# Products with wv, wq and wk: three float32r products of split operands in place of Strassen steps in float32, with weight parts loaded for each pair and the norms on ScalarE

## The chip, the core and the metric

The kernel runs on one core of one Trainium2 chip. A core has five engines that run side by side, each with its own queue of instructions in a fixed order: TensorE (PE, matrix products into the accumulator memory PSUM), VectorE (DVE) and ScalarE (ACT) for elementwise work, GpSimd (POOL) and SyncE (SP). SP, ACT and POOL also start memory transfers (DMA), which run on 16 DMA engines that all queues share. An instruction at the head of its engine's queue that waits for another engine holds up everything behind it.

The metric is device time in microseconds (us) for one execution of the whole program; less is better. All tiles below have 128 partitions, and "512 elements" means 512 per partition.

## The reference

Two layers on x of 64 batches x 256 rows x 512 columns, each a residual with a layer norm. The first is masked attention with 8 heads, the second a product with the adjacency matrix.

```python
def _L0_gnn_ref(x, adj, Wq, bq, Wk, bk, Wv, bv, Wo, bo):
    q = (x @ Wq + bq).reshape(b, n, H, HD)
    k = (x @ Wk + bk).reshape(b, n, H, HD)
    v = (x @ Wv + bv).reshape(b, n, H, HD)
    scores = jnp.einsum('bqhd,bkhd->bhqk', q, k) / jnp.sqrt(jnp.float32(HD))
    scores = scores + (1.0 - adj)[None, None, :, :] * -1000000000.0
    attn = jax.nn.softmax(scores, axis=-1)
    out = jnp.einsum('bhqk,bkhd->bqhd', attn, v).reshape(b, n, d)
    return out @ Wo + bo

def _L1_gnn_ref(x, adj, weight, bias):
    y = jnp.einsum('nm,bmd->bnd', adj, x)
    return jnp.einsum('bnd,do->bno', y, weight) + bias

x = _layernorm(x + _L0_gnn_ref(x, adj, ...), axis=-1)
x = _layernorm(x + _L1_gnn_ref(x, adj, ...), axis=-1)
```

## The kernel before

**Pairs and windows.** The 64 batches are taken as 32 pairs; a pair has 512 rows. The work is laid out in windows. Window w holds the attention of pair w, the three products with wv, wq, wk for pair w+1, and for pair w-1 the projection with wo, the norm, the product with adj, the product with the second layer's weight, and the second norm. x of pair w+2 is turned round in window w. So in the middle of the run one window costs one pair's time. `between(w)` lists the steps of a window in order, `window(w)` puts four attention units between them: a unit is a `scores` call (16 matmul rows, L309, with exponentials L313 on ScalarE and masks L318 on VectorE) and a `values` call (sums L336, values L344, evacuated by ScalarE as zc and vc). Steps put off work with `later`, which `tick` releases a step or more afterwards. A scheduler then fixes the order on every engine; in the first window TensorE and VectorE keep the order as written, in the last TensorE does.

**Products.** Every product of 512 x 512 x 512 (with wv, wq, wk, wo and the second weight) is done in seven Strassen steps (`SEVEN`, `block_product`, L231). A step is four float32 matmuls of 128x128 with 256 columns; the trace shows each of these as two instructions. The sums that Strassen needs are made on VectorE: `weight_sums` once for each weight, `row_sums` (L191) for x, for the attention's output and for the second layer's input. Results are put together by `assembled`: ScalarE evacuates the first of two contributions (L276 for q and k, L288 for v), VectorE adds the others (L263; L414 onto the residual r). All weights stay in memory.

**The product with adj** (`adj_x`, L453) is not Strassen: r is split into two parts, hl and ys, in float32r, a format that TensorE takes in a single pass. ScalarE makes the first part (L438), VectorE the rest (L439).

**Norms.** `stats` on VectorE (L385, L386), `rstd_of` (L391 on VectorE, then a power on GpSimd, L393), and one step later `normed`: four VectorE instructions of 512 elements for each layer (L400), subtract the mean and multiply. After the first layer's norm hl and ys follow, after the second the output is stored (L403) and the next r is loaded.

**Loads.** x of each pair comes in four chunks, each of four transfers of 64 KB in pieces of 128 bytes (L83, on SP), so that VectorE's 32x32 transposes (L249) finish the turn; the first pair is turned by TensorE (L246). r is one transfer of 1 MB a pair (L88).

**Buffers.** PSUM has four banks for attention (`ps_at`) and four for products (`ps_mm`). A Strassen product holds one bank through most of its steps and a second for a part of them.

Of the kernel before, what the change touches and what calls it, by code (L numbers as in the profile page):

```python
# [21 lines left out]
F32R = mybir.dt.float32r  # L22
AF = mybir.ActivationFunctionType
# [5 lines left out]
EPS = 1e-5  # L29
MASKED = -1000000000.0  # L30
# [10 lines left out]
def fast(tc, x, adj, wq, bq, wk, bk, wv, bv, wo, bo, w1, b1, out):  # L41
# [20 lines left out]
    xpool = pool("xp", 1)  # L62
    two = pool("two", 2)
# [8 lines left out]
    XC, R, XT, Q, K, V, E, SM, O, HL, Y, ST = ({} for _ in range(12))  # L72

    def load_x(p, i):


        if p < NP:
            t = XC[p, i] = xpool.tile([P, D], F32, name=f"x{i}")
            if p == 0:
                nc.sync.dma_start(t, xc[p, i % 2, i // 2])  # L80
            else:
                for q in range(4):
                    nc.sync.dma_start(t[q * 32:(q + 1) * 32].rearrange("i (m j) -> i m j", j=32), xb[p, i, q])  # L83
# [8 lines left out]
    for i in range(4):  # L92
        load_x(0, i)
    ident = cpool.tile([P, P], F32, name="ident")
# [36 lines left out]
    weights("v", wv, "hl", nc.scalar)  # L131

    nc.scalar.activation(small.tile([P, 1], F32, name="table"), ones[:, 0:1], AF.Exp)
    weights("q", wq, "e0", nc.sync)
    bq_s, bk_s = by_partition(bq, "bq"), by_partition(bk, "bk")
    weights("k", wk, "e1", nc.sync)
# [100 lines left out]
    def x_t(p, i):  # L237
        if i == 0:
            t = two.tile([P, NC, DC, 2, P], F32, name="xT")
            XT[p] = dict(t=t, **blocks(t[:, :, 0:2], t[:, :, 2:4]))  # L240
        t = XT[p]["t"]
        xs = XC.pop((p, i))
        if p == 0:
            pt = ps_mm.tile([P, DC, P], F32, name="mm")
            for d in range(DC):
                nc.tensor.transpose(pt[:, d, :], xs[:, d * P:(d + 1) * P], ident)  # L246
            nc.scalar.activation(t[:, i // 2, :, i % 2, :], pt, AF.Copy)
        else:
            nc.vector.transpose(t[:, :, i].rearrange("p c b i -> p b c i"),  # L249
                                xs.rearrange("p (b c i) -> p b c i", b=2, c=NC))  # L250
        load_x(p + 1, i)

    def x_sums(p, i):
        row_sums(XT[p], sums_of("xs"))
# [10 lines left out]
    def q_or_k(p, i, is_k):  # L265
        T, b = (K, bk_s) if is_k else (Q, bq_s)
        pm = block_product("qk"[is_k], i, XT[p], W["qk"[is_k]], True)

        def out(g, c):
            if (p, g) not in T:  # L270
                T[p, g] = qk.tile([P, NC, 2, 2, P], F32, name="kT" if is_k else "qT")
            return T[p, g][:, c].rearrange("p a b i -> p a (b i)")

        def first(to, pm, g):
            for a in range(2):
                nc.scalar.activation(to[:, a], pm[:, a], AF.Identity, bias=b[:, 2 * g + a:2 * g + a + 1])  # L276

        assembled(i, pm, out, first)

    def v_rows(p, i):  # L280
        pm = block_product("v", i, XT[p], W["v"], False)

        def out(g, c):
            if (p, g) not in V:
                V[p, g] = four.tile([P, NC, 2, HF], F32, name="v")
            return V[p, g][:, c]

        assembled(i, pm, out, lambda to, pm, g: nc.scalar.activation(to, pm, AF.Copy))  # L288

    def q_cols(p, i):  # L290
        q_or_k(p, i, False)

    def k_cols(p, i):
        q_or_k(p, i, True)
# [6 lines left out]
    def scores(p, u):  # L301
        g, b = UNITS[u]
        for kc in range(NC):

            sc = [ps_at.tile([P, 2, N], F32, name="at") for s in range(2)]
            for a in range(2):
                for s in range(2):
                    r = slice(s * HD, (s + 1) * HD)
                    nc.tensor.matmul(sc[s][:, a, :], K[p, g][r, kc, a, b, :], Q[p, g][r, :, a, b, :],  # L309
                                     start=True, stop=True)  # L310
# [15 lines left out]
    def values(p, u):  # L326
# [13 lines left out]
        for a in range(2):  # L340
            for kc in range(NC):
                for h in range(4):
                    col = h * HD + a * 32
                    nc.tensor.matmul(at[h * 32:(h + 1) * 32, a, :], V[p, g][:, kc, b, col:col + 32],  # L344
# [5 lines left out]
    def divided(p, u, vc, zc):  # L350
# [7 lines left out]
        rs = one.tile([P, N], F32, name="rs")  # L358
# [29 lines left out]
    def rstd_of(p, layer):  # L388
# [3 lines left out]
        rstd = ST[p, layer, "r"] = small.tile([P, 4], F32, name="rstd")  # L392
        nc.gpsimd.tensor_tensor(rstd, ve, power, op=OP.pow)  # L393

    def normed(p, layer):
        mv, rstd = ST.pop((p, layer)), ST.pop((p, layer, "r"))
        for b in range(2):
            for c in range(NC):
                i = 2 * b + c
                nc.vector.tensor_scalar(R[p][:, b, c, :], R[p][:, b, c, :], mv[:, i, 0:1], rstd[:, i:i + 1],  # L400
                                        op0=OP.subtract, op1=OP.mult)
            if layer:
                nc.sync.dma_start(outr[p, b], R[p][:, b])  # L403
            elif b == 0:
                for half in range(2):
                    split(p, b, half)
# [20 lines left out]
    def split(p, b, half):  # L427
# [13 lines left out]
    def adj_x(p, i):  # L441
# [16 lines left out]
        if p < NP - 2 and b == 0:  # L458
            later(1, split, p, 1, half)
# [13 lines left out]
    def by_batch(p, layer, b, lo, hi):  # L473
        if b == 0:
            if (p - NP) % 2 == layer:
                PART[p, layer] = two.tile([P, NC, DC, 2, P], F32, name="xT").rearrange("p c (h k) b i -> p (c h) k (b i)", k=2)
            else:
                PART[p, layer] = sums_of("yx"[layer] + "s")
        PART[p, layer, b] = row_sums(blocks(lo, hi, b), PART[p, layer][:, :, :, b * P:(b + 1) * P])

    def part(p, layer, b, i):
# [6 lines left out]
        if i >= 5:  # L488
# [9 lines left out]
            later(1, finished, p, layer, b, c, mv, rstd)  # L498

    def finished(p, layer, b, c, mv, rstd):  # L500
        r = R[p][:, b, c]
        nc.vector.tensor_scalar(r, r, mv[:, 0:1], rstd, op0=OP.subtract, op1=OP.mult)  # L502
        if layer:
            nc.sync.dma_start(outr[p, b, :, c], r)
        elif c == 0:
            for half in range(2):
                split(p, b, half)
# [25 lines left out]
    def between(w):  # L533
# [5 lines left out]
        both = lambda m, n: [s for pair in zip(m, n) for s in pair] if m and n else m + n  # L539
# [234 lines left out]
```

## Time and profile before

| | |
|---|---|
| median of 3 runs | 2680.01 us (2677.47 to 2680.05) |
| the profiled execution, its own time | 2678.74 us |
| its span, first to last instruction | 2676.9 us |
| granted TensorE clock, mean | 0.996 |
| a middle window, 1010.21 to 1092.29 us | 82.08 us |
| in it: TensorE, VectorE, ScalarE, GpSimd busy | 82.08, 62.01, 25.44, 4.24 us |
| in it: DMA engines busy, traffic | 18%, 39 GB/s |
| transfers of the program: SP's queue, ACT's queue | 105.69 MB, 1.05 MB |

Busy time is the time in which an engine has at least one instruction running. Instructions of one engine overlap at their ends, so what one costs in a stream is the distance from its start to the next start, which is shorter than its duration. L numbers are lines of the kernel before. In lists of groups, the arrow names what is written and what is read, and "x512" says how many there are; in a timeline the first two columns are start and length, and brackets hold idle time before the row and what ended it. A window of DMA traffic by stages showed 379 GB/s in the stretch from 4 to 10 us, where the first x and weights load. The trace has no transfer from POOL's queue.

### The profile page before, as it was taken

What the parts mean: (1) busy time and instruction counts of PE and PEld (TensorE: products, weight loads), DVE (VectorE), ACT (ScalarE), POOL (GpSimd) and SP (SyncE); (2) the same over time, 40 slices, a digit from 0 to 9 for tenths busy, and PEclk for the clock granted to TensorE, in tenths of its full rate; (3) what the DMA queues carried; (4) which work ended last, traced back from release to release, by engine and by line L of the source; (5) the groups of instructions that cost most, each with busy time, mean ns of one, the idle gap of its engine ahead of it and who ended that gap; (6) DMA issues with size and microseconds to landing.
All of it is one profiled execution on the core that took longest, in us unless ns stands there. A gap on an engine that the chain in (4) does not pass through costs nothing.

```text
span 2676.9 us, 42203 instructions
## 1 busy us (share of the span) xinstructions
PE 2647.6 (99%) x17190; PEld 2167.0 (81%) x17190; DVE 2002.2 (75%) x3315; ACT 818.7 (31%) x1670; POOL 140.6 (5%) x340
## 2 busy tenths in 40 slices
PE   9999999999999999999999999999999999999987
PEld 7788888888888888888888888888888888888866
DVE  5777777777877777777777777787777777777777
ACT  3333332333323333323333233332233332333221
POOL 0000000000000000000000000000000000000001
PEclk9999999999999999999999999999999999999998
DMA  6210122201212102222012220122210122200010
GB/s 166 36 42 9 46 48 48 48 10 39 48 48 48 32 16 48 48 48 47 6 44 48 48 48 23 26 48 48 48 44 9 45 48 48 48 9 25 32 40 25
DMA packets 304583, 109.49 MB, mean 41 GB/s; under 512 B 265472, under 2 KB 270848, under 8 KB 304384
## 3 DMA queue, kind: packets, MB, share of 16 engines
q1 hardware_dynamic: 303296, 105.69, 16.6%
q8 instruction: 137, 2.24, 0.3%
q10 hardware_dynamic: 1088, 1.05, 0.1%
q14 instruction: 62, 0.51, 0.1%
HBM read 73.14 MB, written 33.55 MB: 40 GB/s over the span
## 4 chain that ended last, share of the span: by engine, by line
PE 95%; DVE 3%; DMA 1%; issue 0%; POOL 0%; ACT 0%; ACTq 0%; POOLq 0%; DVEq 0%; SPq 0%
PE mm L231 71%; PE at L309 9%; PE at L344 8%; PE mm L453 5%; PE at L336 3%; DVE e L318 1%; DVE st L491 0%; POOL rstd L497 0%; DVE r L502 0%; DMA hl<-in_L_gnn_Wv_dram 0%; DMA hl<-in_L_gnn_Wo_dram 0%; DMA r<-in_x_dram 0%; DVE r L376 0%; DVE o L360 0%; DVE r L486 0%
## 5 line engine op out<-in xcount | busy, mean ns | idle before, releaser
L318 DVE TENSOR_TENSOR e<-e,adjT 128x1024 f32<-128x1024 f32 x256 | 303.2, 1215 | 53.4 <-ACT e L313 53.4
L263 DVE TENSOR_TENSOR r<-r,mm 128x512 f32<-128x512 f32 (+1 forms) x204 | 133.2, 654 | 229.5 <-PE mm L231 229.1
L313 ACT ACTIVATE e<-at 128x512 f32<-128x512 f32 x512 | 264.8, 602 | 58.8 <-PE at L309 58.5
L276 ACT ACTIVATE kT<-mm,bk 128x256 f32<-128x256 f32 x256 | 107.5, 470 | 495.5 <-PE mm L231 495.5
L309 PE MATMUL at<-qT,kT 64*128 64x256 f32 x2048 | 257.2, 389 | 0.0
L231 PE MATMUL mm<-wo,o 128*128 128x256 f32 x1024 | 243.8, 380 | 3.2 <-DVE o L360 2.5
L309 PEld LDWEIGHTS at<-qT,kT 64*128 64x128 f32 x2048 | 190.7, 186 | 67.6 <-issue 53.3
L344 PE MATMUL at<-e,v 128*32 128x256 f32 x4096 | 245.1, 379 | 0.0
L231 PE MATMUL mm<-xT,wq 128*128 128x256 f32 x1024 | 244.8, 382 | 0.2 <-DVE v L263 0.2
L231 PE MATMUL mm<-xT,wk 128*128 128x256 f32 x1024 | 241.6, 379 | 0.0
L231 PE MATMUL mm<-wv,xT 128*128 128x256 f32 x1024 | 241.4, 384 | 0.0
L231 PE MATMUL mm<-w,o 128*128 128x256 f32 x992 | 235.8, 380 | 0.0
L414 DVE TENSOR_TENSOR r<-r,mm 128x512 f32<-128x512 f32 x240 | 163.0, 679 | 83.7 <-PE mm L231 83.7
L231 PEld LDWEIGHTS mm<-wv,xT 128*128 128x128 f32 x1024 | 192.6, 191 | 35.8 <-issue 10.8
L231 PEld LDWEIGHTS mm<-xT,wq 128*128 128x128 f32 x1024 | 192.0, 190 | 35.1 <-issue 9.6
L231 PEld LDWEIGHTS mm<-wo,o 128*128 128x128 f32 x1024 | 194.7, 190 | 30.6 <-issue 2.9
L231 PEld LDWEIGHTS mm<-xT,wk 128*128 128x128 f32 x1024 | 194.5, 190 | 26.4
L231 PEld LDWEIGHTS mm<-w,o 128*128 128x128 f32 x992 | 186.6, 190 | 24.5 <-DVE xT L191 0.3
L344 PEld LDWEIGHTS at<-e,v 128*32 128x32 f32 x4096 | 133.2, 110 | 88.3 <-issue 0.3
L276 ACT ACTIVATE qT<-mm,bq 128x256 f32<-128x256 f32 x256 | 107.0, 469 | 305.0 <-PE mm L231 305.0
L231 PE MATMUL mm<-wv,xs 128*128 128x256 f32 x768 | 184.5, 383 | 0.0
L231 PE MATMUL mm<-xs,wk 128*128 128x256 f32 x768 | 184.5, 383 | 0.0
(130 smaller groups left out, 3746.2 us busy)
## 6 DMA issues: line engine op xcount, KB each, us to landing
r<-in_x_dram SPq DMA_DIRECT2D x32, 1024.0 KB
x<-in_x_dram SPq DMA_DIRECT2D x496, 64.0 KB
out_dram<-r SPq DMA_DIRECT2D x60, 512.0 KB
out_dram<-r SPq DMA_DIRECT2D x8, 256.0 KB
x<-in_x_dram SPq DMA_DIRECT2D x4, 256.0 KB
wv<-in_L_gnn_Wv_dram ACTq DMA_DIRECT2D x3, 256.0 KB
wq<-in_L_gnn_Wq_dram SPq DMA_DIRECT2D x3, 256.0 KB
wk<-in_L_gnn_Wk_dram SPq DMA_DIRECT2D x3, 256.0 KB
```

What stands on the lines that cost most here:

```text
L231: nc.tensor.matmul(pm[:, j, :], left[:, k, j * P:(j + 1) * P], right[:, k, :], start=begins and j == 0 and k == 0, stop=k == 1, skip_group ...
L263: nc.vector.tensor_tensor(to, to, pm, op=OP.add)
L276: nc.scalar.activation(to[:, a], pm[:, a], AF.Identity, bias=b[:, 2 * g + a:2 * g + a + 1])
L309: nc.tensor.matmul(sc[s][:, a, :], K[p, g][r, kc, a, b, :], Q[p, g][r, :, a, b, :], start=True, stop=True)
L313: nc.scalar.activation(e[:, s], sc[s], AF.Exp, scale=qscale)
L318: nc.vector.tensor_tensor(e, e, mask[:, kc:kc + 1, :].to_broadcast([P, 4, N]), op=OP.mult)
L336: nc.tensor.matmul(at[h * 32:(h + 1) * 32, 0, :], ones, sm[:, h % 2, h // 2, :], start=True, stop=True)
L344: nc.tensor.matmul(at[h * 32:(h + 1) * 32, a, :], V[p, g][:, kc, b, col:col + 32], e[kc][:, h % 2, h // 2, :], start=kc == 0, stop=kc == N ...
L414: assembled(i, pm, out, lambda to, pm, half: nc.vector.tensor_tensor(to, to, pm, op=OP.add))
L453: nc.tensor.matmul(pm[:, j, :], hl[:, i, mc, j * P:(j + 1) * P], adjT[:, mc, :], start=mc == 0 and i == 0, stop=mc == NC - 1 and i == 1)
```

## The change

- **v, q, k.** In place of seven Strassen steps, each product is now three float32r products (`part_products`). Both operands are split (`split`): `cut` keeps the upper bits of a number, `low` is the rest, and `diff` is the number minus 4097 times the rest. The three products are cut x cut, low x (4096 low), and diff x (-diff/4096); the first two are summed in one bank (`near`), the third goes to another (`far`). `joined`: ScalarE evacuates near times (1 + 1/4096), VectorE adds far. A product is four groups (j) of 12 matmuls with 512 columns. The first pair's v is done in plain float32 from wv as it is.
- **x.** After VectorE's transpose, `x_parts` splits each chunk: three VectorE instructions and one on ScalarE. There are four buffers for each kind of part, which is one pair's worth. x passes through three staging buffers (`stage`), and the next chunk is loaded when a chunk has been split.
- **Weights.** `split_w` splits wq, wk, wv in the first window, and the parts are stored in a scratch area of device memory (36 stores of 256 KB on SP). For every pair each of the nine parts (1 MB) is loaded again by POOL's queue into a ring of five buffers (`load_w`); three loads are asked for after v's last group, three after q's, three after k's.
- **Norms.** `normed` and `finished` use ScalarE, with scale rstd and bias `less` = -mean x rstd, which one more small VectorE instruction makes.
- **Order.** `between` is rewritten for the groups. `split` of the kernel before is now called `halves`; some tiles share names and buffers differently (`by_batch`, `zc`).

In the built order of a middle window, the third group of scores stands partly between the first matmuls of q's last group, and part of a values call between k's first two parts and its third.

```diff
+    def load_w(name, p, i):
+        if p < NP:
+            t = wring.tile([P, DC, D], F32R, name="wr")
+            nc.gpsimd.dma_start(t, SCRATCH[name, i])
+            WP[name, p, i] = lambda k: t[:, k]
...
+    def split_w(name, k, p=0):
+        parts = high, low, diff = [WP[name, p, i](k) for i in range(3)]
+        split(WP.pop((name, k)), one.tile([P, D], F32, name="vc"), high, low, diff)
+        load_next()
+        nc.scalar.activation(low, low.bitcast(F32), AF.Copy, scale=FINE)
+        nc.scalar.activation(diff, diff.bitcast(F32), AF.Copy, scale=-1 / FINE)
+        for i, part in enumerate(parts):
+            nc.sync.dma_start(SCRATCH[name, i][:, k], part.bitcast(F32))
+
+    def split(a, cut, high, low, diff):
+        nc.vector.tensor_scalar(cut.bitcast(I32), a.bitcast(I32), -int(FINE), None, op0=OP.bitwise_and)
+        nc.vector.tensor_tensor(low, a, cut, op=OP.subtract)
+        nc.scalar.activation(high, cut, AF.Copy)
+        nc.vector.scalar_tensor_tensor(diff, low.bitcast(F32), -(FINE + 1), a, op0=OP.mult, op1=OP.add)
...
+    def x_parts(p, k):
+        XG[p, k], XL[p, k], XD[p, k] = (parts.tile([P, D], F32R, name=n) for n in ("high", "low", "diff"))
+        cut = XC.pop((p, k)) if p else one.tile([P, D], F32, name="vc")
+        split(XF[p, k], cut, XG[p, k], XL[p, k], XD[p, k])
+        if p:
+            load_next()
...
-    def q_or_k(p, i, is_k):
-        T, b = (K, bk_s) if is_k else (Q, bq_s)
-        pm = block_product("qk"[is_k], i, XT[p], W["qk"[is_k]], True)
...
+    def part_products(name, p, j, rows_first):
+        near, far = (ps_mm.tile([P, D], F32, name="mm") for _ in range(2))
+        for i, (xs, to) in enumerate(((XG, near), (XL, near), (XD, far))):
+            for k in range(DC):
+                a, b = xs[p, k], WP[name, p, i](k)
+                left, right = (a, b) if rows_first else (b, a)
+                nc.tensor.matmul(to, left[:, j * P:(j + 1) * P], right, start=k == 0 and i != 1,
+                                 stop=k == DC - 1 and i != 0)
+        return near, far
+
+    def joined(to, near, far, **kw):
+        nc.scalar.activation(to, near, AF.Identity, scale=1 + 1 / FINE, **kw)
+        nc.vector.tensor_tensor(to, to, far, op=OP.add)
...
-                nc.vector.tensor_scalar(R[p][:, b, c, :], R[p][:, b, c, :], mv[:, i, 0:1], rstd[:, i:i + 1],
-                                        op0=OP.subtract, op1=OP.mult)
+                nc.scalar.activation(R[p][:, b, c, :], R[p][:, b, c, :], AF.Identity, scale=rstd[:, i:i + 1],
+                                     bias=less[:, i:i + 1])
...
-        o, v, q, k = z(o_proj, 7, 1.72), a(v_rows, 7, 1.72), a(q_cols, 7, 1.72), a(k_cols, 7, 1.72)
+        o, l, y = z(o_proj, 7, 1.72), z(last, 7, 1.72), z(adj_x, 4, 0.9)
+        v, q, k = a(v_rows, 4, 2.6), a(q_cols, 4, 2.6), a(k_cols, 4, 2.6)
...
+        after_v = load(("q", 0, 2), ("k", 0, 0), ("k", 0, 1))
+        after_q = load(("k", 0, 2), ("v", 1, 0), ("v", 1, 1))
+        after_k = load(("v", 1, 2), ("q", 1, 0), ("q", 1, 1)) + x_all[2:]
...
+        seq = v[:2] + o[:1] + v[2:3] + o[1:2] + v[3:] + after_v + o[2:3] + q[:1] + o[3:4] + q[1:2] + o[4:] + q[2:] + \
+            after_q + k[:1] + y[:2] + x_steps[:2] + k[1:2] + y[2:] + bo_steps[:1] + l[:1] + k[2:3] + bo_steps[1:]
...
+        return seq + l[1:3] + k[3:] + after_k + l[3:]
```

## The prediction

> **What bounds the kernel now.** I read the page's busy shares, then its chain of waits, then one middle stretch of TensorE's timeline, and ScalarE's and VectorE's timelines beside it.
>
> ```profile
> PE 2647.6 (99%) x17190; PEld 2167.0 (81%) x17190; DVE 2002.2 (75%) x3315; ACT 818.7 (31%) x1670; POOL 140.6 (5%) x340
> PE 95%; DVE 3%; DMA 1%; issue 0%; POOL 0%; ACT 0%; ACTq 0%; POOLq 0%; DVEq 0%; SPq 0%
> ```
>
> TensorE is busy almost throughout and 95% of the chain is its own: time goes if its work goes, as long as no wait takes its place.
>
> ```profile
> 1044.09 1.89 PE L231 MATMUL mm<-xT,wq 128*128 128x256 f32 x8
> 1045.82 1.89 PE L231 MATMUL mm<-xs,wq 128*128 128x256 f32 x8
> 1047.64 0.64 PE L336 MATMUL at<-sm,ones 128*32 128x256 f32 x8
> 1048.09 1.91 PE L344 MATMUL at<-e,v 128*32 128x256 f32 x32
> 1049.93 2.00 PE L309 MATMUL at<-qT,kT 64*128 64x256 f32 x16
> 1051.86 1.99 PE L231 MATMUL mm<-xT,wq 128*128 128x256 f32 x8
> ...
> 1058.43 1.11 PE L453 MATMUL mm<-adjT,ys 128*128 128x256 f32 x8
> 1059.38 1.89 PE L231 MATMUL mm<-w,o 128*128 128x256 f32 x8
> ```
>
> The first column is the start; the next start is the true cost. A Strassen step is 8 instructions in 1.726 us: 0.2157 us each, a "slot". Values cost 2.3 us (L336, L344), scores 1.93. The window from 1010.21 to 1092.29 us, which is one pair in steady state, is 82.08 us.
>
> ```profile
> 1043.29 1.29 DVE L385 BATCH_NORM_STATS2 st<-r 128x6 f32<-128x512 f32 x2
> 1044.83 0.17 DVE L391 TENSOR_SCALAR ve<-mv 128x4 f32<-128x4 f32 x1
> 1046.12 1.92 DVE L400 TENSOR_SCALAR r<-r,mv,rstd 128x512 f32<-128x512 f32 x4 [1.12 <-POOL rstd L393]
> ```
>
> ```profile
> 1047.15 0.63 ACT L438 ACTIVATE hl<-r 128x512 fp32r<-128x512 f32 x1 [2.02 <-DVE r L400]
> 1047.69 0.61 ACT L438 ACTIVATE ys<-r 128x512 fp32r<-128x512 f32 x1
> 1050.13 0.60 ACT L347 ACTIVATE vc<-at 128x512 f32<-128x512 f32 x1 [0.82 <-PE at L344]
> 1051.16 2.06 ACT L313 ACTIVATE e<-at 128x512 f32<-128x512 f32 x4 [0.43 <-PE at L309]
> ```
>
> The last o_proj step ends near 1042.4; the norm starts 3.7 us later on VectorE, hl a further 1.0 us later, and ScalarE is free when vc and the exponentials are due.
>
> **TensorE's work.** Before, one product of 512x512x512 is 7 steps, 56 slots. After, it is 3 x 16 matmuls of 512 columns in float32r. What is one of those worth? A float32 row of 256 columns lasts 382 ns and a float32r row of 256 (L453) 281: 101 ns more, so the float32 row streams about 512 columns and the new matmul is one slot, 48 per product. The other bound is twice the float32r spacing of L453, (1059.38-1058.43)/8 = 0.119, so 0.238; that would hold if streaming and not the weight load set the 0.119. I take 0.2157. q and k save 8 slots for 32 pairs each, v for 31; v of the first pair, plain float32, costs 64 slots: 512 + 248 - 8 = 752 slots, **-162.2 us**, 5.18 us per steady window.
>
> **VectorE, per window.** Starts lie 0.60 us apart for 512 elements, 0.46 for L400. Gone: 8 norms 3.7, 4 xs sums 2.4, 9 adds of L263 5.4. New: 12 joins 7.2, 4 cuts 1.9 to 2.4, 8 differences 4.8, two small ones 0.3. Net +2.7, 62.0 to 64.7 us: covered as a total. **ScalarE** loses 16 L276 at 0.42 and 4 L288 at 0.60, gains 12 evacuations, 4 high parts and 8 norms (0.53 apart): 25.4 to about 30 us, covered too. What costs is order, so I walked one steady window of the built order, each instruction at its start spacing, U = 0 where the last o_proj step ends.
>
> - Norm on ScalarE. Its scale needs `less`, which stands on VectorE behind q's third join (q ends at 2.6): ready at 4.3. ScalarE then runs three norms, hl, ys, the fourth norm (0.53 each) before vc, which was ready at 4.9: vc ends at 8.1. The second half of the scores needs vc's bank; TensorE reaches it at 7.2 and waits **0.94** (0 if ScalarE is quicker, 1.5 if slower).
> - The order splits these scores so that their two row halves no longer run together: 0.97 + 2 x 0.86 for 1.93: **0.76** (0 to 0.86).
> - The exponentials then end at 9.8, the masks 11.75, q's join 12.35, sm 13.6; TensorE wants sm at 12.9: **0.75** (0 to 1.5). Five of its 16 value matmuls are pulled forward, which cuts a group of four: **0.43** (0 to 0.46).
> - wk's third part. Five ring buffers hold nine parts, so its 1 MB load waits on POOL's queue until the last q group has used wq's first part, at 9.45; TensorE wants it at 15.0, 5.55 us later. No POOL transfer is in this trace. The nearest rows: the first x transfer, issued 0.75, used at 3.91 (256 KB; at the 379 GB/s of the stretch 4 to 10 us that is 2.5 us fixed, so 1 MB lands in 5.2), and
>
> ```profile
> 1.74 6.61 DMA hl<-in_L_gnn_Wv_dram
> ```
>
>   256 KB beside 2 MB of others: 6.6 us, 8.7 for 1 MB. I take 6.2, nearer the quiet row since nothing else loads then: **0.65** (0 to 3.2). Behind it in POOL's queue stand two more loads and the small `seen`/`acc`, wanted much later. The other loads have 9 us (wq's third part) or more.
> - VectorE's x parts can only be written once the last k group is done (four buffers each), and they stand between the `last` adds: the sixth `last` step waits **0.6** (0 to 1.5); v's last difference is ready some 1 us ahead. o_proj's first step waits 0.1 for a bank.
>
> Together 4.25 us, of 5.18. For 30 steady windows **+127 us**. Start: 36 stores of parts on SP (about 0.45 us each) stand ahead of the second pair's x, and VectorE splits 12 weight quarters (1.7 us each) plus that x; hoisted scores and values hide most. I take **+8** (0 to 15). Tail: each norm is followed by one more small step, **+2** (-2 to +5). Sum, on the profiled execution's 2678.7 (span 2676.9; median of the runs 2680.0): 2678.7 - 162.2 + 127 + 8 + 2 = **2653.5**.
>
> The Trainium skill speaks twice to wk's load. "DMA: Bandwidth & Descriptors", section "Anatomy of one DMA", gives 2.0 us plus bytes over 436 GB/s, an estimate of 4.4 us for 1 MB: no wait, and the sum would be 2634. Against the change, "SBUF — State Buffer", section "SBUF: two separate sides", says that a transfer issued from GpSimd cannot have its descriptors written while VectorE runs a two-port operation. L400 at 0.54 us against 0.68 for L414 may be such a form, but no run here shows that lock; one cut's 0.46 us in front of each wk load would make the sum 2667.
>
> **Rivals.**
> - *The waits are hidden.* Latencies in this walk are guesses of a tenth or two each, and a later order can absorb them: for it, TensorE now loses under 1 us per window although VectorE is 75% busy. If only the unpaired scores, the cut group and 0.5 us remain (1.7 us): 2678.7 - 162.2 + 51 + 5 = 2573.
> - *wk's third part lands late*, slower than before. TensorE stops in every window before k's first difference product. My sum loses its gain at 25.2/30 = 0.84 us more, a landing of 7.05 us; at 8.7 us it is 2.5 more per window: 2729. For: the load starts on demand, and POOL's share is unseen. Against: 379 GB/s was reached here.
> - *x comes late.* Each pair's fourth x chunk (128-byte pieces) loads while 3 MB of parts go over the same engines; VectorE's transpose would block, then ScalarE's high part, then vc. Some 2.5 us per window: 2729. The walk has 1 to 2 us to spare.
> - *The float32r matmul takes 0.238.* 4560 x 0.022 = +100: 2753. Against: L453's 281 ns.
>
> **Chances.** My forecast 0.42, hidden waits 0.20, late wk 0.24, late x 0.08, 0.238 us 0.06. About 0.2%, 5.4 us, is what a measurement of this kernel can tell from no change. My case spreads some 30 us either way: of its 0.42, 0.31 is faster, 0.06 the same, 0.05 slower. Faster 0.51, same 0.07, slower 0.42. Half of the hidden case lies under 2570 and a tenth in all above 2740, so 2570 to 2740 holds 8 in 10; my own case alone is 2622 to 2685.
>
> **What would show it.** TensorE rows of the part products 0.216 us apart (not 0.238). In a middle window, idle before the L428/L393 rows put down to ScalarE's vc, before L420 to VectorE's sm, and before wk's third group to a DMA, about 0.6 us. Norm rows on ScalarE ahead of vc. A window of about 81 us. If TensorE idles under 1 us per window the hidden case is true; if the DMA wait is 1.5 us or more, the late one.

## The result, and the profile after

The changed kernel takes 2921.23 us (median of 4 runs, 2917.71 to 2922.17) against 2680.02 us for the kernel before on the same chip: a ratio of 1.09, 95% interval 1.0881 to 1.0919. It is 241 us slower, where 26 us faster was forecast, and it lies outside the range of 2570 to 2740. The granted TensorE clock of the profiled execution is 0.963 in the mean, where it was 0.996.

The page of the changed kernel: first the busy time of each engine, then the shares of the chain of waits by engine and by line.

```profile
PE 2722.0 (93%) x16406; PEld 2087.8 (71%) x16406; DVE 2087.8 (71%) x3515; ACT 1053.5 (36%) x1838; POOL 304.6 (10%) x616
PE 57%; DVE 15%; DMA 11%; issue 5%; ACT 5%; SPq 4%; POOL 2%; DVEq 0%; POOLq 0%; ACTq 0%
PE mm L345 28%; PE mm L290 14%; DMA x<-in_x_dram 8%; PE at L393 6%; PE mm L539 4%; PE at L428 4%; SPq L85 3%; DVE st L469 3%; DVE e L402 3%; DMA wr<-k 3%; DVE sm L408 2%; ACT r L486 2%; DVE r L332 1%; ACT e L397 1%; DVE r L500 1%
```

TensorE's share of the chain fell from 95% to 57%. The largest entry of anything but TensorE is none of the waits in the forecast's sum, but the loads of x (8%), with SyncE's issues of them (SPq L85, 3%).

To see where the time went I cut every profiled run at two marks: the first values of window 2 (the eighth group of L420 rows; L336 before) and the same place 29 windows later. The tail is what follows.

| | start, to window 2 | one window, mean of 29 | tail | span |
|---|---|---|---|---|
| before | 185.05 | 82.42 | 101.6 | 2676.9 |
| after | 235.02 | 89.04 | 103.3 | 2920.4 |
| difference | +50.0 | +6.62 (x 29 = +192) | +1.7 | +243.5 |

So four fifths are lost in the windows and one fifth at the start. This is the end of one window, all engines in order of their starts (start, length, engine, line, what is written and read, and in brackets the idle time before and what ended it):

```profile
1025.41 0.57 POOL L141 DMA_DIRECT2D wr<-v  x1 [19.39 <-PE mm L345]
...
1026.22 16.64 SPq L85 DMA_DIRECT2D x<-in_x_dram  x16
1026.33 0.53 POOL L141 DMA_DIRECT2D wr<-q  x1 [0.35 <-PE mm L345]
...
1027.25 0.53 POOL L141 DMA_DIRECT2D wr<-q  x1 [0.38 <-PE mm L345]
...
1036.08 1.56 PE L393 MATMUL at<-qT,kT 64*128 64x256 f32 x10
1038.52 0.71 DVE L315 STREAM_TRANSPOSE xT<-x 128x512 f32<-128x512 f32 x1 [4.34 <-DMA x<-in_x_dram]
...
1039.73 0.63 ACT L183 ACTIVATE high<-x 128x512 fp32r<-128x512 f32 x1 [4.79 <-DVE x L181]
...
1040.26 0.58 ACT L431 ACTIVATE vc<-at 128x512 f32<-128x512 f32 x1
...
1040.89 1.65 PE L393 MATMUL at<-qT,kT 64*128 64x256 f32 x6 [3.25 <-ACT vc L431]
...
1042.48 2.07 PE L345 MATMUL mm<-wr,high 128*128 128x512 f32 x4
...
1044.35 1.28 PE L345 MATMUL mm<-wr,low 128*128 128x512 f32 x4
```

Read it backwards from TensorE's 3.25 us of idle time. The last six score rows wait for vc. vc was ready to be copied, but ScalarE takes its instructions in order, and the one ahead, the high part of an x chunk, waits for VectorE, whose transpose waits 4.34 us for x. That chunk is the fourth of its pair: it was asked for at 1026.22, with the three loads of parts (3 MB) beside it. The list of waits has VectorE's wait for x 30 times, 128.2 us in all, up to 5.1 us each.

The wait costs more than its length. Stretches of the same place: stretch, its length, busy time (instructions) of PE, PEld, DVE, ACT and POOL, then the granted TensorE clock, the DMA engines' busy share, GB/s.

```profile
1035.00:1038.00 3.00, 2.64 (x34) 1.47 (x26) 0.00 (x0) 0.00 (x0) 0.00 (x0) 1.00 1.42 225
1038.00:1041.00 3.00, 0.11 (x2) 0.11 (x2) 2.48 (x7) 1.27 (x3) 0.00 (x0) 1.00 0.90 122
1041.00:1044.00 3.00, 3.00 (x10) 1.95 (x11) 3.00 (x9) 2.00 (x4) 0.58 (x1) 0.56 0.54 85
1044.00:1047.00 3.00, 3.00 (x13) 2.43 (x12) 1.90 (x5) 1.20 (x2) 1.75 (x3) 0.87 0.02 3
```

After the idle time the clock is 0.56, then 0.87. Taken by single us from 1041 it is 0.68, 0.50, 0.50, 0.61 and then 1.00: half the clock for 3.4 us, which is 1.7 us of work. The group that starts at 1042.48 takes 1.87 us to the next start, where such a group otherwise takes 0.91; the six score rows take 1.59, where 6 of 16 are 0.72. With the 0.2 of the group at 1044.35 that is 2 us more, most of it the clock's: some 5.3 us a window.

This is not the only place where the clock falls. Length times one minus the granted clock, added up in stretches of 2 us between the two marks, is 78.5 us for the changed kernel, 2.7 a window, and nothing for the kernel before: 28 of the 29 waits for x and 15 of the 28 waits of 1.0 us in the middle of a window are followed by a fall.

The middle of the window is as the forecast walked it. ScalarE and TensorE there:

```profile
1081.18 2.22 ACT L486 ACTIVATE r<-r,less,rstd 128x512 f32<-128x512 f32 x3 [0.38 <-DVE less L478]
1082.01 1.99 PE L393 MATMUL at<-qT,kT 64*128 64x256 f32 x12
1083.31 0.61 ACT L524 ACTIVATE hl<-r 128x512 fp32r<-128x512 f32 x1
...
1083.93 0.73 PE L345 MATMUL mm<-high,wr 128*128 128x512 f32 x2
...
1084.35 0.80 ACT L486 ACTIVATE r<-r,less,rstd 128x512 f32<-128x512 f32 x1
1085.05 0.57 ACT L431 ACTIVATE vc<-at 128x512 f32<-128x512 f32 x1
...
1085.68 1.13 PE L393 MATMUL at<-qT,kT 64*128 64x256 f32 x4 [1.02 <-ACT vc L431]
```

Three norms, hl, ys and the fourth norm stand ahead of vc; TensorE waits 1.02 us, and the scores, cut into 12 and 4 rows, take 1.92 + 1.06 us from start to start in place of 1.93.

### The profile page after: what moved, and what is told of

Its sections match the earlier page's. It is cut to its first block, busy times and chain, and to the rows that moved or that the text cites. A ratio compares the mean times of both kernels' runs of the same rounds, so it can differ in the third digit from the quotient of the medians.

```text
span 2920.4 us, 41961 instructions
## 1 busy us (share of the span) xinstructions
PE 2722.0 (93%) x16406; PEld 2087.8 (71%) x16406; DVE 2087.8 (71%) x3515; ACT 1053.5 (36%) x1838; POOL 304.6 (10%) x616
## 3 DMA queue, kind: packets, MB, share of 16 engines
q10 hardware_dynamic: 544, 1.05, 0.1%
## 4 chain that ended last, share of the span: by engine, by line
PE 57%; DVE 15%; DMA 11%; issue 5%; ACT 5%; SPq 4%; POOL 2%; DVEq 0%; POOLq 0%; ACTq 0%
PE mm L345 28%; PE mm L290 14%; DMA x<-in_x_dram 8%; PE at L393 6%; PE mm L539 4%; PE at L428 4%; SPq L85 3%; DVE st L469 3%; DVE e L402 3%; DMA wr<-k 3%; DVE sm L408 2%; ACT r L486 2%; DVE r L332 1%; ACT e L397 1%; DVE r L500 1%
## 5 line engine op out<-in xcount | busy, mean ns | idle before, releaser
L345 PE MATMUL mm<-high,wr 128*128 128x512 f32 x1024 | 324.7, 434 | 6.5 <-ACT wr L183 6.5
L345 PE MATMUL mm<-diff,wr 128*128 128x512 f32 x1008 | 278.6, 399 | 11.2 <-DMA wr<-k 6.0
L345 PE MATMUL mm<-low,wr 128*128 128x512 f32 x1024 | 288.1, 405 | 0.2 <-ACT wr L173 0.2
L345 PEld LDWEIGHTS mm<-diff,wr 128*128 128x128 f32 x1008 | 191.8, 193 | 66.0 <-DMA wr<-k 12.4
L350 ACT ACTIVATE qT<-mm,bq 128x512 f32<-128x512 f32 x128 | 88.1, 688 | 413.6 <-PE mm L345 413.4
L345 PEld LDWEIGHTS mm<-high,wr 128*128 128x128 f32 x1024 | 187.1, 192 | 70.0 <-issue 32.7
L345 PEld LDWEIGHTS mm<-low,wr 128*128 128x128 f32 x1024 | 201.3, 197 | 46.9 <-ACT wr L173 0.7
L486 ACT ACTIVATE r<-r,less,rstd 128x512 f32<-128x512 f32 x240 | 178.7, 804 | 95.4 <-DVE less L478 95.4
L183 ACT ACTIVATE high<-x 128x512 fp32r<-128x512 f32 x124 | 74.9, 627 | 299.7 <-DVE x L181 183.2
L345 PE MATMUL mm<-wr,high 128*128 128x512 f32 x496 | 174.3, 477 | 6.2 <-ACT high L183 6.2
```

The source lines that it names most:

```text
L345: nc.tensor.matmul(to, left[:, j * P:(j + 1) * P], right, start=k == 0 and i != 1, stop=k == DC - 1 and i != 0)
L350: nc.scalar.activation(to, near, AF.Identity, scale=1 + 1 / FINE, **kw)
L486: nc.scalar.activation(R[p][:, b, c, :], R[p][:, b, c, :], AF.Identity, scale=rstd[:, i:i + 1], bias=less[:, i:i + 1])
```

## The experiments

Each kernel is the changed one with the edit named, timed beside the kernel before (2678 to 2680 us in each series). no_reload, both_no_reload, start_plain, no_stores and start_bare leave out work that the result needs; they only tell what it costs. Leaving out lines moves line numbers by a few. All results in one table; the interval is that of the ratio to the kernel before.

| kernel | median us | ratio, 95% interval | start | one window | tail |
|---|---|---|---|---|---|
| after | 2921.2 | 1.0881 to 1.0919 | 235.0 | 89.04 | 103.3 |
| x_early | 2823.5 | 1.0523 to 1.0558 | 238.9 | 85.54 | 102.4 |
| no_reload | 2719.2 | 1.0141 to 1.0175 | 218.8 | 82.68 | 101.2 |
| norms_dve | 2901.9 | 1.0820 to 1.0856 | 233.6 | 88.11 | 108.2 |
| both | 2724.7 | 1.0153 to 1.0187 | 237.2 | 82.01 | 107.8 |
| x_norm1 | 2751.1 | 1.0254 to 1.0288 | 238.7 | 82.91 | 106.5 |
| both_no_reload | 2652.1 | 0.9884 to 0.9917 | 228.7 | 79.83 | 106.3 |
| start_plain | 2982.0 | 1.1112 to 1.1149 | 229.6 | 91.35 | 101.7 |
| no_stores | 2913.1 | 1.0857 to 1.0893 | 229.1 | 88.81 | 103.3 |
| start_bare | 2904.4 | 1.0819 to 1.0855 | 211.9 | 89.37 | 103.4 |
| best_a | 2710.5 | 1.0100 to 1.0134 | 236.6 | 81.61 | 105.4 |
| best_b | 2699.0 | 1.0059 to 1.0093 | 225.4 | 81.58 | 105.7 |
| best_c | 2700.2 | 1.0062 to 1.0096 | 227.5 | 81.57 | 105.6 |
| best_d | 2713.5 | 1.0108 to 1.0142 | 235.5 | 81.63 | 108.8 |
| best_e | 2699.8 | 1.0059 to 1.0093 | 223.6 | 81.56 | 108.6 |
| best_f | 2705.6 | 1.0082 to 1.0115 | 233.2 | 81.57 | 103.9 |

### Is it the fourth x chunk, and why is it late?

x_early gives x a fourth staging buffer, so that the fourth chunk of a pair, too, is asked for a window ahead; xT keeps one buffer in place of two:

```diff
-    xpool = pool("xp", 2)
-    stage = pool("stage", 3)
+    xpool = pool("xp", 1)
+    stage = pool("stage", 4)
...
-    for _ in range(3):
+    for _ in range(4):
         load_next()
...
-        x_all = x_steps[:2] + [s for i in range(4) for s in x_parts_[i:i + 1] + x_steps[i + 2:i + 3]]
+        x_all = [s for i in range(4) for s in x_steps[i:i + 1] + x_parts_[i:i + 1]]
...
```

> The changed kernel with a fourth staging buffer for x chunks (and one xT buffer instead of two, each chunk turned just before it is cut), so that all four chunks of a pair are asked for a window ahead. Theory 1 (the fourth chunk is asked for too late): VectorE's 128 us of waits for x on DMA fall below 15 us, the wait of the scores for vc at the window's end goes with them, no stretch of the window has a granted clock under 0.9, and 30 windows lose about 5 us each: 2921 - 150 = 2771 us (2750 to 2800). Rival 2 (x is only the first of several late things there: ScalarE's high part or the group's cut value product would hold the end anyway): the wait moves to another name and less than 70 us is gained, above 2850 us.

VectorE's wait for x on DMA is gone, but the gain is 98 us, 3.5 a window, between the two forecasts. The clock still falls, for 0.9 us a window in place of 2.7. Timeline of a window of x_early, just behind the place of the old wait:

```profile
1014.72 2.93 ACT L486 ACTIVATE r<-r,less,rstd 128x512 f32<-128x512 f32 x4 [2.56 <-DVE less L478]
1015.15 1.07 PE L345 MATMUL mm<-wr,diff 128*128 128x512 f32 x4
1017.55 1.05 ACT L350 ACTIVATE v<-mm 128x512 f32<-128x512 f32 x2
1018.18 1.99 PE L290 MATMUL mm<-wo,o 128*128 128x256 f32 x8 [1.96 <-ACT v L350]
```

Now the second layer's four norms on ScalarE stand ahead of the copies of v, whose PSUM banks the first o_proj step needs: 1.96 us in every window (24 times, 47.0 us, between 400 and 2400 us). While x was late, TensorE reached that place later and this wait was not there. A gain of 5.3 less 2.0 is the 3.5 measured, to 0.2.

no_reload keeps the late request and takes the other traffic away:

```diff
-            t = wring.tile([P, DC, D], F32R, name="wr")
-            nc.gpsimd.dma_start(t, SCRATCH[name, i])
-            WP[name, p, i] = lambda k: t[:, k]
+            WP[name, p, i] = WP["v", 1, i]
```

> Leaves out: the reloading of the weights' parts after the first pair; every later product uses wv's parts, so 3 x 3 MB of loads per window are gone and nothing else. If the fourth x chunk is late because its small pieces share the DMA engines with 3 MB of parts, its wait (4.3 us per window) goes and the time falls to about 2921 - 30 x 5 = 2770 us or a little below. If it is late because it is issued late and takes four issues of 1.04 us, most of the wait stays: above 2860 us. If streaming costs the matmuls anything, the groups of four f32r matmuls come closer than 0.92 us; I expect them unchanged.

VectorE then never waits for an x chunk on DMA, so the request is late only together with 3 MB of parts on the same DMA engines; either remedy suffices. The windows gain 6.4 us, 1.4 more than the 5 us expected for the wait, and the start 16. The gain is not x's alone: wk's part cannot be late either, and the falls of the clock cost 0.3 us a window in place of 2.7. Groups of four f32r matmuls stay 0.91 us apart: the loads do not slow the matmuls. The traffic of the changed kernel between 1020 and 1045 us by queue (packets, MB, share of the 16 engines' time) shows why the small one suffers:

```profile
q1 hardware_dynamic: 8448, 1.05, 40.7%
q0 software_dynamic: 432, 3.15, 36.6%
```

1.05 MB of x in pieces of 128 bytes takes more engine time than 3.15 MB of parts.

### The norms on ScalarE

```diff
-                nc.scalar.activation(R[p][:, b, c, :], R[p][:, b, c, :], AF.Identity, scale=rstd[:, i:i + 1],
-                                     bias=less[:, i:i + 1])
+                nc.vector.tensor_scalar(R[p][:, b, c, :], R[p][:, b, c, :], rstd[:, i:i + 1], less[:, i:i + 1],
+                                        op0=OP.mult, op1=OP.add)
```

norms_dve is this edit alone, `finished` included; both is x_early with it; x_norm1 is x_early with it in the second layer only.

> The changed kernel with its norms back on VectorE (one tensor_scalar of multiply and add per 512 columns instead of ScalarE's activation). By the trace the norms ahead of vc make the scores wait 1.02 us in the middle of a window and 0 to 0.8 us elsewhere, so 30 to 50 us at most would come back: 2870 to 2890 us; the end-of-window wait for x stays at 4.3 us. Rival: VectorE, at 71% busy, gets 3 us more per window and gives back what ScalarE frees: 2915 us or more.

> The changed kernel with the fourth staging buffer (x chunks asked for a window ahead) and with both layers' norms on VectorE. With x in time alone a window takes 85.5 us; in it TensorE waits 1.96 us for v's ScalarE copies and 1.01 us for vc, both behind ScalarE's four norms, and lets the scores go unpaired (about 1 us). Theory (the norms on ScalarE are the second cost, which the late x hid): these 3.5 to 4 us go, 81.5 to 82 us a window, 2823 - 105 to 120 = 2703 to 2718 us. Rival (the norms are worth the 19 us that they were worth with x late): 2800 us. Second rival (VectorE, with 3 us more a window, makes sm or the joined parts late): above 2740 us.

> The fourth staging buffer, with only the second layer's norms on VectorE; the first layer's stay on ScalarE. If the wait of the first o step for v's copies comes from the second layer's norms and the unpaired scores at the window's middle from the first layer's, the 1.96 us go and the 1.01 us stay: 85.5 - 2 = 83.5 us a window, 2763 us (2750 to 2775). If both waits hang on either, it is near 2823 or near 2710 us.

Alone the edit gains 19 us, less than the 30 to 50 expected; with x in time it gains 98.8 (2823.5 to 2724.7). The two edits together gain 196.5 where their single gains add up to 117: each hid the other's cost. Of the 98.8, the second layer's norms are worth 72 (x_norm1, 2.6 us a window, a little more than the 2.0 expected), the first layer's 26 (with `finished`, which x_norm1 leaves on ScalarE). Per window, the 3.5 us are the 1.96 for v, 0.74 of the 1.01 for vc, and 0.9 of the clock's falls, which shrink to 0.06. `both` missed its range by 7 us, and the place is seen in it. GpSimd and TensorE around wk's third part:

```profile
1019.33 1.08 POOL L448 TENSOR_TENSOR seen<-rz,z 128x8 f32<-128x8 f32 x1 [5.00 <-DVE rz L441]
1020.49 0.20 POOL L449 TENSOR_TENSOR acc<-acc,seen 128x8 f32<-128x8 f32 x1
1020.95 0.62 POOL L141 DMA_DIRECT2D wr<-k  x1 [0.25 <-issue]
...
1026.14 1.20 PE L345 MATMUL mm<-diff,wr 128*128 128x512 f32 x4 [0.56 <-DMA wr<-k]
```

The load is issued behind two tiny additions that wait for VectorE; issued at 1020.95, it lets TensorE go on 5.2 us later, 0.56 us late. best_a, below, moves them.

> Leaves out: the reloading of parts after the first pair (later products use wv's parts); with the fourth staging buffer and all norms on VectorE. It tells what the part products alone are worth: 48 slots of 0.228 us against 56 of 0.2157 per product are 3.4 us a window less TensorE work than the kernel before, so 82.1 - 3.4 = 78.7 us a window if nothing waits, and 218.8 + 29 x 78.7 + 101 = 2602 us (2590 to 2640). Rival: VectorE's added work for parts keeps windows above 81 us, above 2670 us.

Without the reloading a window is 79.8 us: the new products are worth 2.6 us a window where almost nothing waits, 0.8 less than the 3.4 expected by slots. That makes 33 us in 29 windows; with a start 10 us later and a tail 5 us longer than the expectation assumed, it is 2652 and not 2602. Against `both`, the streaming of parts still costs 2.2 us a window even where x is in time and the norms are off ScalarE: 0.78 is the wait for wk's third part and 0.52 that for sm, which both_no_reload has not; the rest I have not placed.

### The start

> Leaves out: the splitting of the three weights into parts at the start, their scaling and their stores; the parts' buffers are filled with the plain weights by DMA, and what is streamed later is the plain weights too. Theory: the 52 us by which window 1 begins later than in the kernel before come from the splits and from the x chunks of pair 1 that stand behind them; without them window 1's first values begin at 110 to 130 us in place of 155, and the time is 2921 - 25 to 45 = 2876 to 2896 us. Rival: the start is held by the loads of w1 and wo and by pair 1's x alone, and less than 10 us is gained.

```diff
-            SCRATCH[name, i] = scratch.tile([P, DC, D], F32, name=f"{name}{i}")
+            SCRATCH[name, i] = STREAMED[name].rearrange("(c p) e -> p c e", p=P)
...
-        split(WP.pop((name, k)), one.tile([P, D], F32, name="vc"), high, low, diff)
...
-        for i, part in enumerate(parts):
-            nc.sync.dma_start(SCRATCH[name, i][:, k], part.bitcast(F32))
+        for part in parts:
+            nc.gpsimd.dma_start(part, STREAMED[name][k * P:(k + 1) * P])
```

The kernel was slower, where 25 to 45 us less was expected, and the run separates little. It kept as many bytes and turned the later loads into pieces of 2 KB in place of 8 KB: 207.6 MB of them took 36.0% of the DMA engines between 400 and 2400 us, against 212.2 MB in 29.1%, they landed in 7.9 to 9.1 us in place of 6.8 to 7.8, and windows rose to 91.4 us. Only its start can be read: 5 us earlier.

no_stores leaves out the two lines of the stores and streams contiguous rows, `"(p c) e -> p c e"`; start_bare leaves out the splits as well:

```diff
...
-        split(WP.pop((name, k)), one.tile([P, D], F32, name="vc"), high, low, diff)
+        nc.scalar.activation(high, WP.pop((name, k)), AF.Copy)
         load_next()
-        nc.scalar.activation(low, low.bitcast(F32), AF.Copy, scale=FINE)
-        nc.scalar.activation(diff, diff.bitcast(F32), AF.Copy, scale=-1 / FINE)
-        for i, part in enumerate(parts):
-            nc.sync.dma_start(SCRATCH[name, i][:, k], part.bitcast(F32))
```

> Leaves out: the 36 stores of weight parts (9.4 MB); the splits stay, and what is streamed later is the plain weights, in loads of the same size and of contiguous rows. Theory (the start is bound by the DMA engines, which move 22.5 MB in the first 100 us against 12.4 MB before, at 320 to 400 GB/s, so that pair 1's x comes last): 9.4 MB at 350 GB/s are 27 us, and window 2's first values begin at 205 to 215 us in place of 235: 2921 - 20 to 30 = 2891 to 2901 us, with windows of 89 us as they were. Rival (VectorE's and ScalarE's splitting is the start's cost): less than 8 us is gained.

> Leaves out: the splits of the three weights and the 36 stores; each weight quarter is copied once by ScalarE into one buffer that serves as all three parts, and what is streamed later is the plain weights in contiguous rows. The stores alone were worth 6 us of the start's 50 (window 2's first values at 229 us in place of 235), the splits with the stores kept as loads of the same bytes also 6. Theory (either the DMA engines' 9.4 MB or VectorE's 36 passes of splitting ahead of pair 1's x parts holds the start, so only both together count): window 2's first values begin at 195 to 210 us, and the time is 2921 - 25 to 40 = 2881 to 2896 us. Rival (the start is held by pair 1's x loads and by the order around them, whatever the weights cost): less than 12 us is gained, 2909 us or more.

Without the stores alone the start is 6 us shorter (20 to 30 were expected), without the splits alone (start_plain) 5, without both 23: the DMA engines and the passes of VectorE and ScalarE hold it side by side, and each covers for the other. Stretches of the start, first the kernel before, then the changed kernel, then start_bare:

```profile
60.00:80.00 20.00, 20.00 (x139) 14.84 (x128) 13.69 (x22) 7.39 (x16) 0.81 (x4) 1.00 0.27 50
80.00:100.00 20.00, 19.59 (x127) 15.38 (x125) 15.99 (x19) 7.74 (x17) 0.41 (x2) 1.00 0.11 17
```

```profile
60.00:80.00 20.00, 11.41 (x90) 5.95 (x94) 13.07 (x21) 4.98 (x10) 0.81 (x4) 0.74 0.76 225
80.00:100.00 20.00, 16.66 (x96) 9.02 (x89) 9.87 (x13) 5.41 (x10) 0.00 (x0) 0.73 0.19 31
```

```profile
60.00:80.00 20.00, 15.34 (x78) 8.66 (x79) 16.34 (x28) 6.00 (x11) 0.85 (x2) 0.83 0.48 104
80.00:100.00 20.00, 20.00 (x130) 15.21 (x129) 14.97 (x21) 7.16 (x13) 1.83 (x3) 1.00 0.18 61
```

In the changed kernel TensorE is idle 12 of 40 us there and runs at a clock of 0.73 in the rest; the kernel before is busy 39.6 of these 40 us at 1.00. The total of start_bare gained only 17, since its windows were 0.33 us longer, 9.6 us in 29. In them its clock's falls cost 92.2 us and the changed kernel's 78.5, which is enough to account for it.

### Towards a faster version

best_a is x_early with `normed` (not `finished`) on VectorE and with the first edit below; best_b adds the second and third. best_c to best_f change orders at the start: `window(0)` moved inside the hand-made order (best_c); the stores of parts by `nc.gpsimd`, with that (best_d) or without (best_e); best_d with SyncE in the hand-made order too, so that both `load_r`, w1 and wo come after pair 1's x, and with the biases on GpSimd's queue (best_f).

```diff
-        nc.gpsimd.tensor_tensor(seen, rz, z1, op=OP.add)
-        nc.gpsimd.tensor_tensor(acc, acc, seen, op=OP.add)
+        nc.vector.tensor_tensor(seen, rz, z1, op=OP.add)
+        nc.vector.tensor_tensor(acc, acc, seen, op=OP.add)
...
-        nc.vector.tensor_tensor(t1, b12, b11, op=OP.subtract)
+        nc.gpsimd.tensor_tensor(t1, b12, b11, op=OP.subtract)
...
-        nc.sync.dma_start(t, b.partition_broadcast(P))
+        nc.scalar.dma_start(t, b.partition_broadcast(P))
...
         window(-1)
+        window(0)
-    for w in range(NP - 1):
+    for w in range(1, NP - 1):
```

> The fourth staging buffer; the norms of the windows on VectorE, those of the last pairs on ScalarE; and the two small additions of the running sum of seen values on VectorE instead of GpSimd, where they stand ahead of the issue of wk's third part (issued 1.3 us late behind them, and TensorE waits 0.56 to 1.3 us for it). Expected: a window at 80.6 to 81.0 us in place of 81.65, a tail of 103 us in place of 108: 2725 - 30 x 0.8 - 5 = 2696 us (2685 to 2705). If the third part's load is what is slow, not its issue, the windows stay at 81.6 us and the time at 2719 us.

> The kernel best_a with two things more at the start: the Strassen sums of w1 and wo on GpSimd instead of VectorE, where they wait for w1's last quarter among the splits of wq (TensorE stands 2.65 and 1.99 us behind), and the loads of bv, bo and b1 on ScalarE's queue instead of SyncE's, where they take 7.9 us of issue ahead of w1 and of the weights' quarters. Expected: 5 to 10 us less than best_a, all of it before 60 us. Rival: GpSimd's eight sums hold up its own queue, the loads of parts, and what is gained is lost by 160 us.

> The kernel best_b with the order of TensorE and VectorE in window 0 as the program has it, instead of one made by the scheduler: VectorE cuts all four x chunks of pair 1 before the masks of pair 0, and TensorE runs pair 1's v product between the first scores and the first values. If the late x parts of pair 1 with scores and values let in between them are what costs the start its low clock (0.74 between 60 and 100 us), 8 to 20 us come back against best_b. If the x chunks are late by their loads, the fixed order waits longer: 5 to 15 us more than best_b.

> The kernel best_c with the 36 stores of parts on GpSimd's queue instead of SyncE's. In best_c TensorE stands 15 us between 60 and 80 us for the high parts of pair 1's x, whose chunks SyncE issues between 52 and 72 us, each behind stores that wait for ScalarE's scaling. If the stores ahead of them are what makes the chunks late, the v product of pair 1 begins 5 to 12 us earlier and the time is 2688 to 2695 us. If the bytes are what makes them late (the DMA engines were 0.9 to 1.06 busy between 40 and 80 us), nothing is gained: 2698 us or more.

> The kernel best_b (window 0 in the scheduler's order) with the stores of parts on GpSimd's queue. By the theory that the order between the x parts and the scores decides here, less is gained than with the order of the program: 2694 to 2699 us.

> The kernel best_d with SyncE's order of the program too: what is not needed before 90 us (4 MB: the two residual loads, w1 and wo) is asked for after pair 1's x chunks, and the loads of bv, bo and b1 go to GpSimd's queue. If the bytes hold the start, 4 MB at 380 GB/s are 10 us: 2680 to 2688 us, window 2's first values at 205 to 215 us. If VectorE's 36 passes of splitting hold it, it is as best_d within 3 us.

best_a gains 14 of the 29 us expected: the wait for wk's third part is gone but for one (1.9 us between 400 and 2400 us, where `both` had 18.7), yet a window only falls by 0.4, to 81.6 in the mean, and scores and values still wait 0.3 for vc and 0.7 for sm. best_b gains 11.5 more, all at the start, a little over the forecast. The other four gained nothing on best_b: no order tried at the start was worth anything. best_d lost 13 us to best_c; in it the scheduler put wo's loads ahead of wk's quarters (VectorE waited 3.53 us for one at 42.8 us). best_f took 4 MB out of the stretch, gained 8 us on best_d, between its two forecasts, and stayed 6.7 us behind best_b. Its stretch, and what VectorE waits for in it:

```profile
60.00:80.00 20.00, 6.17 (x13) 4.19 (x14) 7.84 (x13) 2.49 (x4) 0.54 (x1) 0.50 1.00 199
```

```profile
66.11 0.71 DVE L313 STREAM_TRANSPOSE xT<-x 128x512 f32<-128x512 f32 x1 [8.04 <-DMA x<-in_x_dram]
```

The DMA engines are full (1.00) at 199 GB/s: x's small pieces with the last stores and the first loads of parts. I read this so: asking for x earlier does not help while these bytes are there. No run took them away on top of best_f.

No version that does the whole work beat the kernel before. The best, best_b, is 7.6% faster than the changed kernel and 0.6 to 0.9% slower than before: its windows are 0.84 us shorter (24 us in 29), its start 40 us later, its tail 4 us longer.

## Why the prediction was wrong

- **The x rival.** This is the step that failed first: the sum has no term for x, and the runs show 5.3 us a window. The forecast named the mechanism exactly, "VectorE's transpose would block, then ScalarE's high part, then vc", and gave it 0.08, with the remark that the walk "has 1 to 2 us to spare". That slack was a guess on a transfer whose landing no row of the walk gave. The chunk was asked for at 1026.2, and VectorE came to it at 1034.2, 8 us later; beside 3 MB it took 12.3. The price, 2.5 us a window, was short of the 3.25 us idle and left out the 2 us behind it, most of them the clock's.
- **Waits do not add.** Sum and rivals were priced one by one. With x late, norms cost 0.9 us a window (89.04 to 88.11); with x in time, 3.5. "o_proj's first step waits 0.1 for a bank" is the second step that failed: the walk was of x in time, and there the wait is 1.96, behind the second layer's norms on ScalarE, which the walk did not set ahead of v's copies. It is 0 only while x is late.
- **The slot.** 0.2157 us was taken, 0.228 measured (0.91 to 0.92 for a group of four), a little past the middle between the two bounds. On 4560 matmuls that is 56 us of the 162. The argument from the rows' lengths could at most show that both stream 512 columns, not that a start-to-start distance follows from it. TensorE's gain per window is 3 x (56 x 0.2157 - 48 x 0.228) = 3.4 us, not 5.18.
- **The start.** +8 forecast, +50 measured. The step "hoisted scores and values hide most" counted SyncE's issues and VectorE's passes, and not bytes: the program moved 22.45 MB in its first 100 us in place of 12.42. Removing stores and splits gave back 23 us, better places for the sums and biases 11 in another version; the rest, including window 1's own late chunk, was not separated.
- **vc behind the norms** was right in its mechanism: 0.94 forecast, 1.02 measured; the scores cut in two 0.76, measured 1.05. The closeness of the first is partly luck: a norm took 0.71 us of ScalarE rather than 0.53, so vc ended 8.9 us after the last o_proj step and not 8.1, but TensorE came to it 0.8 us later, too.
- **sm**: 0.75 forecast, 0.26 measured. **wk's third part**: 0.65 forecast, 6.0 us in the whole run measured, with landings of 6.8 us (6.2 assumed); TensorE was itself late by then. With the other waits gone it came to 0.78 a window (18.7 us in 24), close to the forecast, and it went when two additions left GpSimd's queue: the place in the queue, not the transfer, was short. **The sixth `last` step** did not wait. **The tail**, +2, was +1.7. The seven waits of the walk add up to 4.23, not 4.25, which changes nothing.
- The estimate of 4.4 us for 1 MB by the Trainium skill ("DMA: Bandwidth & Descriptors", section "Anatomy of one DMA") was below the 6.8 to 7.8 us measured with other transfers under way. The lock between VectorE and GpSimd's descriptors that the forecast quoted was shown by no run here.

The windows add up so: -3.4 for the products, +5.3 for x, +2.1 for vc and the cut scores, and 2.6 left to reach +6.6. Of these, sm is 0.26, the cut values call 0.5 (0.43 + 0.95 + 1.43 us in x_early's timeline in place of 2.3), wk's third part 0.2, and the falls of the clock that do not follow the wait for x 0.9; the remaining 0.7 I have not placed.

## What to carry to other kernels

Before new traffic is put on the DMA engines, list every load that is asked for on demand in the same stretch, and compare the distance from its issue to its first reader with its landing under that load: here one more staging buffer, in place of one of xT's two, took the whole wait away. An engine with a fixed order passes a late input on to everything behind it, so a slack instruction (here the high part of x for a later pair) must not stand ahead of one that TensorE waits for (vc). And test two suspected waits together as well as singly: the later one is invisible until the earlier one is gone.

## What the hardware showed that was not expected

- A float32r matmul of 512 columns takes longer than the float32 row of 256 that was held to stream as long: 0.228 us against 0.2157. 256 columns of float32r took 0.119 us; if streaming sets both, that is 0.010 us and 0.426 ns a column, but no run here separates the two parts. "TensorE: Matmul & The Clock Gate", section "Wait — 56ns, not 53.3ns?", of the Trainium skill gives N columns at 2.4 GHz plus about 2.5 ns, measured on another type: the float32 rows of 256 columns agree with its 215.7 ns for 512, the float32r rows of 512 are 12 ns above it.
- The clock fell to 0.50 for a fixed time, and not after every wait. Between its marks the trace of the changed kernel has 44 falls, 42 of 3.4 us and two of 6.8. They start whole multiples of 3.413 us from one another: those at 420.1, 464.5, 508.9 and 553.3 lie 13 such steps apart. So what a wait costs depends on where it lies: after 1.02 us for vc the clock stayed at 1.00 at 1085.7 and fell at 1266.6, and in x_early it was 0.65 in the 4 us from 1054, at a wait of 1.01 us, and 1.00 after one of 1.96 at 1018.2. The same page's section "What's actually happening" speaks of an idle window of about 3.4 us; the length agrees, but TensorE need not be idle through it: in the 3.41 us before the fall at 1055.2 in x_early its busy time was 2.40.
- ScalarE's activation over 512 elements took 587 ns as a plain copy, 688 with a bias for each partition, 804 with a scale and a bias for each. "ScalarE: Activation LUTs", section "What ACT_TABLE_LOAD costs", gives about 93 ns for each such operand; the steps here are 101 and 116. The norm reads SBUF and the other two PSUM, though; copies from SBUF (into float32r) took 618 to 627, and against these the norm's two operands are some 91 each. The forecast took the copy's price for the norm.
